# A conditional residual block on one core: beta of every fourth group by DMA, b2 by GpSimd, and a later load of x

## The chip, the cores and the metric

The kernel runs on one core of a Trainium2 chip. The metric is the device time of one execution in microseconds. The kernel before takes 313.89 us (median of 3 runs, 313.76 to 314.14). A core has five engines that work side by side, each on its own queue of instructions: PE (TensorE, matmuls and transposes), DVE (VectorE), ACT (ScalarE), Pool (GpSimd) and SP (SyncE), which here only issues DMAs. An instruction waits for semaphores that other engines or DMAs raise; what stands behind it in the same queue waits with it.

## The reference

x has 128 batches of 128 rows by 512 columns. Each batch b has an id v (0 to 9) that picks one of ten sets of weights W1, b1, W2, b2, gamma, beta. For each batch:

```
h   = relu(x @ W1[v] + b1[v])            # 128 x 128
y   = x + h @ W2[v] + b2[v]              # 128 x 512
out = x + (y - mean(y)) * rsqrt(var(y) + 1e-5) * gamma[v] + beta[v]
```

Mean and variance go over the 512 columns. All data are float32.

## The kernel before

**Tiling.** The 128 rows of a batch are the partitions. x is loaded in groups of four batches (G = 4, 32 groups, 1 MB each) into a pool of four buffers (`xp`); out is stored in pairs of batches (512 KB each). W1, W2 and the rows of gamma, beta and b2, spread over all partitions (`gamma_b`, `beta_b`, `b2_b`), stay in SBUF.

**One batch.** PE transposes x (L218), multiplies by W1 (L241) and by W2 (L258). ACT copies the transposed x (L222), stages the batch's W1 (L209), applies relu (L249), and sums the squares (L288). DVE adds up y and its row sum (`residual`, L273), subtracts the mean and multiplies by gamma (`scale`, L322), and multiplies by the reciprocal deviation and adds a tile o (`finish`, L331). Pool makes two sums: r = x + b2 (`add_b2`, L228), which `residual` reads, and o = x + beta (`add_beta`, L235), which `finish` reads and overwrites with the result. SP issues the load of x (`load_x`, L68) and the store of o (`store`, L335).

**Three ways to add b2.** `b2_by_matmul` (the first four batches, and every batch with b % 4 == 1 that is not done by DVE; 22 in all): one more matmul into y's accumulation (L257), and `residual` reads x itself. `b2_by_vector` (b % 8 == 5 from 13 to 109; 13 in all): an add on DVE before `residual` (L271). All others (93): Pool makes r.

**Order.** One Python loop runs over i; with b = i - 3 it issues, in this order: the load of x three groups ahead (at the first batch of a group), transposes of batch b + 3, `add_b2(b + 2)`, `add_beta(b)`, the W1 product of b + 2, the W2 product of b + 1, then DVE's work for b and the two batches before it: `finish` and `store` are three batches behind `residual`. `keep` fixes that order on each engine. The stores are outside of it: the tile scheduler puts them where it thinks fit among SP's other instructions. The language ids are read into registers of each engine once per group (`lid`).

**Buffers.** r has four (`rp`), a pair's o five (`op`), x four, y five PSUM banks (`p_y`). A tile of a pool takes the buffer of the tile that stands as many places before it as the pool has buffers, and waits until that one's readers (for o: its store) are done.

**End.** The last four batches are finished in `tail`, in an order written out by hand. Pool has the last five big instructions of its own there: for batches 123 and 124 a multiplication by gamma (L384) and an add (L386), for 125 an add. The queue of Pool before them ends with the adds of beta for batches 125 to 127. The stores of single batches follow in order on SP (`store_last`, L389).

Of the kernel before, what the change touches and what calls it, by code (L numbers as in the profile page):

```python
# [8 lines left out]
FP = mybir.dt.float32  # L9
# [3 lines left out]
ALU = mybir.AluOpType  # L13
ET = mybir.EngineType
PSUM = bass.MemoryType.PSUM

P = 128
G = 4
# [6 lines left out]
def cond_resid_kernel(ctx: ExitStack, tc: tile.TileContext, x, itok, W1, b1, W2, b2, gamma, beta, out):  # L25
# [8 lines left out]
    nc = tc.nc  # L34
    B, S, H = x.shape
    L, _, A = W1.shape
    KC = H // P
    NG = B // G
# [5 lines left out]
    def keep(ins):  # L44

        engine = ins.ins.engine
        if engine in last:
            tc.add_manual_dep(ins.ins, last[engine], behind, reason="kept order")
        last[engine] = ins.ins.name
        return ins  # L50
# [1 line left out]
    const = ctx.enter_context(tc.tile_pool(name="const", bufs=1))  # L52
    xp = ctx.enter_context(tc.tile_pool(name="xp", bufs=4))
    rp = ctx.enter_context(tc.tile_pool(name="rp", bufs=4))
    op = ctx.enter_context(tc.tile_pool(name="op", bufs=5))
    tp = ctx.enter_context(tc.tile_pool(name="tp", bufs=2))
    wp = ctx.enter_context(tc.tile_pool(name="wp", bufs=3))
    st = ctx.enter_context(tc.tile_pool(name="st", bufs=6))
# [5 lines left out]
    xs = {}  # L64

    def load_x(g):
        t = xp.tile([P, G, H], FP, tag="x", name=f"x_{g}")
        keep(nc.sync.dma_start(out=t, in_=x[g * G : (g + 1) * G].rearrange("b s h -> s b h")))  # L68
        xs[g] = t

    def xb(b):
        return xs[b // G][:, b % G, :]
# [27 lines left out]
    for l in range(0, L, 5):  # L100
        keep(
            nc.sync.dma_start(
                out=w1e[:, l : l + 5].rearrange("p l k a -> p l (k a)"),
                in_=W1[l : l + 5].rearrange("l (p k) a -> p l (k a)", k=KC),
# [4 lines left out]
    def load_w1(k):  # L109
        keep(  # L110
            nc.sync.dma_start(out=w1[:, :, k, :], in_=W1[:, k * P : (k + 1) * P, :].rearrange("l p a -> p l a"))
        )

    for l in range(0, L, 5):
        keep(
            nc.sync.dma_start(
                out=w2[:, l * H : (l + 5) * H].rearrange("p (l h) -> p l h", l=5),
                in_=W2[l : l + 5].rearrange("l a h -> a l h"),
# [48 lines left out]
    beta_b = const.tile([P, L * H], FP, name="beta_b")  # L167
# [14 lines left out]
    lids, xT, w1s, hT, rs, os, ys, ssqs, nmeans, rstds = {}, {}, {}, {}, {}, {}, {}, {}, {}, {}  # L182
    phs, pxs, sums = {}, {}, {}

    def lid(b, engine):
        g = b // G
        if (g, engine) not in lids:
            loads, vals = nc.values_load_multi_w_load_instructions(
                lang[0:1, g * G : (g + 1) * G],
                engines=[engine],  # L190
                min_val=0,
                max_val=L - 1,
                skip_runtime_bounds_check_because="clamped on the chip to 0..L-1 above",
            )
            for ins in loads:
                keep(ins)
            lids[g, engine] = vals
        return lids[g, engine][b % G]

    def b2_by_matmul(b):  # L200
        return b < 4 or (b % 4 == 1 and not b2_by_vector(b))

    def b2_by_vector(b):
        return b % 8 == 5 and 8 <= b < B - 16

    def stage_w1(b):
        w1s[b] = wp.tile([P, KC, A], FP, tag="w1s", name=f"w1s_{b}")
        src = (w1e if b < EARLY else w1).rearrange("p l k a -> p (l k a)")[:, bass.ds(lid(b, ET.Activation) * (KC * A), KC * A)]
        keep(nc.scalar.copy(w1s[b].rearrange("p k a -> p (k a)"), src))  # L209

    def transpose_x(b):
        pxs[b] = p_x.tile([P, KC, P], FP, tag="xT", name=f"pxT_{b}")
        for k in range(KC):
            if b < EARLY:
                cols = xb(b).rearrange("s (p k) -> s k p", k=KC)[:, k, :]
            else:
                cols = xb(b)[:, k * P : (k + 1) * P]
            keep(nc.tensor.transpose(pxs[b][:, k, :], cols, ident))  # L218

    def copy_xT(b):  # L220
        xT[b] = tp.tile([P, KC, P], FP, tag="xT", name=f"xT_{b}")
        keep(nc.scalar.copy(xT[b], pxs.pop(b)))  # L222

    def add_b2(b):
        if not b2_by_matmul(b) and not b2_by_vector(b):
            rs[b] = rp.tile([P, H], FP, tag="r", name=f"r_{b}")
            v = lid(b, ET.Pool)
            keep(nc.gpsimd.tensor_tensor(rs[b], xb(b), b2_b[:, bass.ds(v * H, H)], ALU.add))  # L228

    def add_beta(b):  # L230
        g, j = divmod(b, 2)
        if j == 0:
            os[g] = op.tile([P, 2, H], FP, tag="o", name=f"o_{g}")
        v = lid(b, ET.Pool)
        keep(nc.gpsimd.tensor_tensor(os[g][:, j, :], xb(b), beta_b[:, bass.ds(v * H, H)], ALU.add))  # L235

    def down(b):
        phs[b] = p_h.tile([P, P], FP, tag="h", name=f"ph_{b}")
        for k in range(KC):
            keep(  # L240
                nc.tensor.matmul(  # L241
                    phs[b], lhsT=w1s[b][:, k, :], rhs=xT[b][:, k, :], start=(k == 0), stop=(k == KC - 1)
                )
            )
        del xT[b], w1s[b]

    def relu(b):
        hT[b] = tp.tile([P, P], FP, tag="hT", name=f"hT_{b}", bufs=6)
        keep(nc.scalar.activation(hT[b], phs.pop(b), AF.Relu, bias=b1T[:, bass.ds(lid(b, ET.Activation), 1)]))  # L249

    def up(b):
        v = lid(b, ET.PE)
        ys[b] = p_y.tile([P, H], FP, tag="y", name=f"py_{b}")
        m = b2_by_matmul(b)
        if m:
            pick_b = pick[:, bass.ds(v + 2 * L, 1)].to_broadcast([96, P])
            keep(nc.tensor.matmul(ys[b], lhsT=pick_b, rhs=parts[:96, :], start=True, stop=False))  # L257
        keep(nc.tensor.matmul(ys[b], lhsT=hT[b], rhs=w2[:, bass.ds(v * H, H)], start=not m, stop=True))  # L258
        del hT[b]
# [5 lines left out]
    def residual(b):  # L265
        r = rs.pop(b) if b in rs else xb(b)
        if b % 2 == 0:
            sums[b // 2] = st.tile([P, 2], FP, tag="sum", name=f"sum_{b // 2}")
        if b2_by_vector(b):
            v = lid(b, ET.DVE)  # L270
            keep(nc.vector.tensor_tensor(ys[b], ys[b], b2_b[:, bass.ds(v * H, H)], ALU.add))  # L271
        keep(
            nc.vector.scalar_tensor_tensor(ys[b], ys[b], 1.0, r, ALU.mult, ALU.add, accum_out=col(sums, b))  # L273
        )
# [28 lines left out]
    def rstd_1(g):  # L303
        y0s[g] = p_s.tile([P, 6], FP, tag="s", name=f"stat_{g}")
        keep(nc.vector.reciprocal(y0s[g][:, 0:2], sds[g]))  # L305
# [32 lines left out]
    def on(b):  # L338
        return 0 <= b < B
# [151 lines left out]

    for i in range(3, B + U):
        b = i - U - 1
        if b > 0 and b % G == 0 and b // G + 3 < NG:
            load_x(b // G + 3)
        if i == 5:
            load_x(3)
        if i in (4, 6, 8, 10):
            load_w1((i - 4) // 2)
        if i == 4:  # L500
            up(2)
        if i == 5:
            up(3)
        if i > 3 and on(i):
            transpose_x(i)
        if b <= E:
            add_b2(b + 2)
            add_beta(b)
        if i > 4 and on(i - 1):
            down(i - 1)  # L510
        if i > 3 and on(i):
            copy_xT(i)
        if i > 4 and on(i + 1):
            stage_w1(i + 1)
        if i > 4 and on(i - 1):
            relu(i - 1)
        if i > 5 and on(i - U):
            up(i - U)


        g, half = divmod(b, 2)
        p = g - 1
        mine, old = 0 <= p < B // 2, 0 <= p - 1 < B // 2
        if b == E:
            add_b2(b + 3)
            add_beta(b + 1)
            add_b2(b + 4)
            for n in range(b + 2, B):
                add_beta(n)
        if b > E:  # L530
            tail(b)
        elif half == 0:
            if on(b):
                residual(b)
            if mine:
                rstd_1(p)
                scale(2 * p)
            if on(b):
                negative_mean(b)
            if mine:  # L540
                rstd_2(p)
            if old:
                finish(2 * p - 1)
                store(p - 1)
            if mine:
                rstd_3(p)
        else:
            if on(b):
                residual(b)
            if mine:  # L550
                rstd_4(p)
                scale(2 * p + 1)
            if on(b):
                negative_mean(b)
            if mine:
                finish(2 * p)
        if 0 <= b <= E:
            square(b)
            if half == 1:
                deviation(g)  # L560

        for n, engine in ((i + 3, ET.Activation), (i - U + 3, ET.PE), (b + 1, ET.DVE), (b + 5, ET.Pool)):
            if on(n):
                lid(n, engine)
# [37 lines left out]
```

## Time and profile before

| | |
|---|---|
| median of 3 runs | 313.89 us (313.76 to 314.14) |
| the profiled execution | 313.83 us, of which the span of its instructions 312.1 us |
| granted TensorE clock, mean | 0.99 |
| PE busy | 300.5 us (96%), 1869 instructions |
| DVE busy | 297.3 us (95%), 945 |
| ACT busy | 285.4 us (91%), 724 |
| Pool busy | 280.1 us (90%), 234 |
| DMA | 75.49 MB, 242 GB/s over the span |

Busy is the time in which at least one instruction of an engine ran, and the share is an average over the whole span, the first 20 us of loading and the last 15 us included. Instructions of one engine overlap in their pipelines: a Pool add lasts 1274 ns in the mean, but the next starts 1233 ns after it. So the distance from start to start tells what an instruction costs, and the duration when its result is there. A DMA's time counts from its issue to its landing. L12 is line 12 of the kernel before; from L55 on the lines of the changed kernel have other numbers (L228 becomes L229, L235 becomes L254, L335 becomes L354).

### The profile page before, as it was taken

To read this page: it belongs to the slowest core of one execution; us is meant where nothing else is said; L and a number is where in the kernel's file an instruction comes from. 1 tells how busy PE (TensorE), PEld (TensorE's weight loads), DVE (VectorE), ACT (ScalarE), POOL (GpSimd) and SP (SyncE) were. 2 spreads that over 40 slices of the span, in tenths; PEclk is the share of its full clock that TensorE was granted. 3 is DMA by queue.
4 is the path that set the end of the run, shared out by engine and by line. 5 is a ranking of instruction groups with operands and counts; after the bars stand their busy time and mean duration, and the time that the engine had idled before them with its cause. 6 is when DMAs were issued, how large, how long until landed. Compare 5 with 4: busy or idle time off the path is not lost.

```text
span 312.1 us, 7096 instructions
## 1 busy us (share of the span) xinstructions
PE 300.5 (96%) x1869; PEld 223.8 (72%) x1869; DVE 297.3 (95%) x945; ACT 285.4 (91%) x724; POOL 280.1 (90%) x234
## 2 busy tenths in 40 slices
PE   8999999999999999999999999999999999999970
PEld 3567787777777767777777777777777777777740
DVE  6677999999999999999999999999999999999995
ACT  3878999999999999999999999999999999999982
POOL 1319978999999999999999999999999999999963
PEclk9999999999999999999999999999999999999995
DMA  6999998767776777667666567576666667633234
GB/s 209 387 387 352 326 339 275 238 229 226 236 250 225 255 265 269 242 231 270 257 227 226 210 238 253 213 272 269 232 232 198 232 247 239 244 134 138 88 149 168
DMA packets 42313, 75.49 MB, mean 242 GB/s; under 512 B 1785, under 2 KB 6916, under 8 KB 42274
## 3 DMA queue, kind: packets, MB, share of 16 engines
q1 hardware_dynamic: 42214, 75.00, 68.6%
q8 instruction: 15, 0.25, 0.3%
q14 instruction: 24, 0.20, 0.2%
q10 hardware_dynamic: 60, 0.05, 0.1%
HBM read 41.49 MB, written 33.55 MB: 240 GB/s over the span
## 4 chain that ended last, share of the span: by engine, by line
PE 91%; DVE 5%; ACT 1%; issue 1%; DVEq 1%; DMA 1%; ACTq 0%
PE ph L241 36%; PE py L258 34%; PE pxT L218 18%; PE py L257 1%; PE row L175 1%; DVE py L273 1%; DVE gamma_b L180 1%; DVE py L322 1%; DVE o L331 1%; DMA rows<-in_L_cond_b_dram 1%; ACT sq L366 0%; DVEq L597 0%; ACT n L382 0%; DVE left L156 0%; DVE left L154 0%
## 5 line engine op out<-in xcount | busy, mean ns | idle before, releaser
L235 POOL TENSOR_TENSOR o<-x,beta_b 128x512 f32<-128x512 f32 x128 | 161.6, 1274 | 12.8 <-ACT beta_b L178 9.2
L241 PE MATMUL ph<-xT,w1s 128*128 128x128 f32 x1024 | 135.6, 275 | 0.5 <-ACT w1s L209 0.5
L258 PE MATMUL py<-w,hT 128*128 x256 | 131.1, 594 | 0.0
L228 POOL TENSOR_TENSOR r<-x,b_b 128x512 f32<-128x512 f32 x93 | 118.5, 1274 | 11.5 <-DMA x<-in_x_dram 9.2
L241 PEld LDWEIGHTS ph<-xT,w1s 128*128 128x128 f32 x1024 | 124.7, 192 | 2.4 <-ACT w1s L209 1.0
L218 PEld LDWEIGHTS pxT<-ident,x 128*128 128x128 f32 x512 | 65.5, 148 | 64.9 <-issue 44.8
L322 DVE SCALAR_TENSOR_TENSOR py<-py,nmean,gamma_b 128x512 f32<-128x512 f32 x126 | 93.8, 745 | 0.2 <-issue 0.2
L331 DVE SCALAR_TENSOR_TENSOR o<-py,rstd,o 128x512 f32<-128x512 f32 x122 | 91.0, 746 | 0.0
L288 ACT ACTIVATE sq<-py,sum 128x512 f32<-128x512 f32 x124 | 85.3, 688 | 1.4 <-DVE py L273 1.3
L222 ACT COPY xT<-pxT 128x512 f32<-128x512 f32 x128 | 73.8, 577 | 9.8 <-PE pxT L218 6.3
L218 PE MATMUL pxT<-ident,x 128*128 128x128 f32 x512 | 77.4, 274 | 0.0
L209 ACT COPY w1s<-w 128x512 f32 x112 | 69.5, 621 | 0.0
L273 DVE SCALAR_TENSOR_TENSOR py<-py,r 128x512 f32<-128x512 f32 x93 | 64.6, 694 | 1.3 <-PE pxT L218 0.6
L249 ACT ACTIVATE hT<-ph,b1T 128x128 f32<-128x128 f32 x128 | 47.4, 370 | 1.0 <-PE ph L241 1.0
L258 PEld LDWEIGHTS py<-w,hT 128*128 128x128 f32 x256 | 40.6, 192 | 2.4 <-ACT hT L249 0.7
L273 DVE SCALAR_TENSOR_TENSOR py<-py,x 128x512 f32<-128x512 f32 x35 | 24.4, 697 | 1.6 <-ACT sq L288 0.6
L288 ACT ACTIVATION_READ_ACCUMULATOR sq<-py,sum 128x1 f32 x124 | 25.7, 208 | 0.0
L299 ACT ACTIVATE sd<-ssq,eps 128x2 f32<-128x2 f32 x62 | 18.3, 296 | 2.1
L279 DVE TENSOR_SCALAR nmean<-sum 128x1 f32<-128x1 f32 x128 | 19.5, 152 | 0.1
L305 DVE RECIPROCAL stat<-sd 128x2 f32<-128x2 f32 x62 | 13.0, 210 | 1.0 <-ACT sd L299 1.0
L273 DVE DVE_READ_ACCUMULATOR py<-py,r 128x1 f32 x93 | 13.4, 144 | 0.0
L317 DVE RECIPROCAL rstd<-stat 128x2 f32<-128x2 f32 x62 | 10.4, 168 | 0.0
(56 smaller groups left out, 120.6 us busy)
## 6 DMA issues: line engine op xcount, KB each, us to landing
out_dram<-o SPq DMA_DIRECT2D x61, 512.0 KB, 3.9
x<-in_x_dram SPq DMA_DIRECT2D x30, 1024.0 KB, 5.8
w1e<-in_L_cond_W_dram SPq DMA_DIRECT2D x2, 1280.0 KB, 8.7
w<-in_L_cond_W_dram SPq DMA_DIRECT2D x2, 1280.0 KB
w<-in_L_cond_W_dram SPq DMA_DIRECT2D x4, 640.0 KB, 15.2
x<-in_x_dram SPq DMA_DIRECT2D x4, 512.0 KB, 8.4
out_dram<-o SPq DMA_DIRECT2D x6, 256.0 KB, 2.0
rows<-in_L_cond_beta_dram ACTq DMA_DIRECT2D x1, 20.0 KB
```

The costliest lines, as they stand in the source:

```text
L209: keep(nc.scalar.copy(w1s[b].rearrange("p k a -> p (k a)"), src))
L218: keep(nc.tensor.transpose(pxs[b][:, k, :], cols, ident))
L222: keep(nc.scalar.copy(xT[b], pxs.pop(b)))
L228: keep(nc.gpsimd.tensor_tensor(rs[b], xb(b), b2_b[:, bass.ds(v * H, H)], ALU.add))
L235: keep(nc.gpsimd.tensor_tensor(os[g][:, j, :], xb(b), beta_b[:, bass.ds(v * H, H)], ALU.add))
L241: nc.tensor.matmul(phs[b], lhsT=w1s[b][:, k, :], rhs=xT[b][:, k, :], start=(k == 0), stop=(k == KC - 1))
L249: keep(nc.scalar.activation(hT[b], phs.pop(b), AF.Relu, bias=b1T[:, bass.ds(lid(b, ET.Activation), 1)]))
L258: keep(nc.tensor.matmul(ys[b], lhsT=hT[b], rhs=w2[:, bass.ds(v * H, H)], start=not m, stop=True))
L273: nc.vector.scalar_tensor_tensor(ys[b], ys[b], 1.0, r, ALU.mult, ALU.add, accum_out=col(sums, b))
L288: nc.scalar.activation(sq, ys[b], AF.Square, bias=col(sums, b), scale=-float(H), accum_out=col(ssqs, b))
L322: nc.vector.scalar_tensor_tensor(ys[b], ys[b], col(nmeans, b), gamma_b[:, bass.ds(v * H, H)], ALU.add, ALU.mult)
L331: nc.vector.scalar_tensor_tensor(o, ys.pop(b), rstds[g][:, j : j + 1], o, ALU.mult, ALU.add)
```

## The change

- In every fourth group (q % 4 == 3, up to group 27; seven groups) Pool makes no o = x + beta. Instead SP issues four DMAs of 256 KB that copy the four batches' beta rows from `beta_b` into a tile `od` of the whole group (`fill_beta`), five batches ahead; two batches ahead, Pool issues one DMA that adds the 1 MB of x onto it (`add_x`). `finish` and `store` use the halves of `od` like two tiles o.
- `od` has one buffer, and `op` has four instead of five.
- b2 is added by matmul in the first four batches alone (4 instead of 22), by DVE where b % 16 == 5, from 21 to 101 (6 instead of 13), and by Pool in all others (118 instead of 93).
- The load of x three groups ahead is issued at the third batch of a group instead of the first.

```diff
-    op = ctx.enter_context(tc.tile_pool(name="op", bufs=5))
+    op = ctx.enter_context(tc.tile_pool(name="op", bufs=4))
+    od = ctx.enter_context(tc.tile_pool(name="od", bufs=1))
...
     def b2_by_matmul(b):
-        return b < 4 or (b % 4 == 1 and not b2_by_vector(b))
+        return b < 4
 
     def b2_by_vector(b):
-        return b % 8 == 5 and 8 <= b < B - 16
+        return b % 16 == 5 and 8 <= b < B - 16
...
+    def beta_by_dma(q):
+
+        return q % 4 == 3 and q < NG - 2
+
+    def fill_beta(q):
+
+        o = od.tile([P, G, H], FP, tag="od", name=f"od_{q}")
+        os[2 * q], os[2 * q + 1] = o[:, 0:2, :], o[:, 2:4, :]
+        for j in range(G):
+            v = lid(q * G + j, ET.SP)
+            keep(nc.sync.dma_start(out=o[:, j, :], in_=beta_b[:, bass.ds(v * H, H)]))
+        return o
+
+    def add_x(q, o):
+        keep(nc.gpsimd.dma_start(out=o, in_=xs[q], accum_op=ALU.add))
+
     def add_beta(b):
         g, j = divmod(b, 2)
+        if beta_by_dma(b // G):
+            return
         if j == 0:
             os[g] = op.tile([P, 2, H], FP, tag="o", name=f"o_{g}")
...
     for i in range(3, B + U):
         b = i - U - 1
-        if b > 0 and b % G == 0 and b // G + 3 < NG:
+        if b > G and b % G == 2 and b // G + 3 < NG:
             load_x(b // G + 3)
...
         if i > 3 and on(i):
             transpose_x(i)
+        q, at = divmod(b + 5, G)
+        if at == 0 and beta_by_dma(q):
+            filled = fill_beta(q)
+        q, at = divmod(b + 2, G)
+        if at == 0 and beta_by_dma(q):
+            add_x(q, filled)
         if b <= E:
             add_b2(b + 2)
             add_beta(b)
```

In the changed kernel's built program, SP's instructions of one such group stand in this order (group 7; tile o_g is the pair of batches 2g and 2g + 1, od_q the four of group q):

```
load   x_8      waits for PE and Pool (the last readers of x_4: beta of batch 19 on Pool)
store  od_3     first half, waits for DVE
store  od_3     second half, waits for DVE
registers: the language ids of group 7
fill   od_7     waits for both stores of od_3
fill   od_7
fill   od_7
store  o_8      waits for DVE
fill   od_7
```

## The prediction

> **What bounds the kernel now.** I read the page first (busy shares, the chain that ended last, the costliest groups), then the timelines of PE and Pool in the middle and at the end, then the DMA view of single stretches. Busy shares and chain:
>
> ```profile
> PE 300.5 (96%) x1869; PEld 223.8 (72%) x1869; DVE 297.3 (95%) x945; ACT 285.4 (91%) x724; POOL 280.1 (90%) x234
> ...
> PE 91%; DVE 5%; ACT 1%; issue 1%; DVEq 1%; DMA 1%; ACTq 0%
> ```
>
> Four engines look full, but the chain that ended last is 91% PE. Matmul starts of the down-to-output product (PE timeline; start, us, engine, line):
>
> ```profile
> 73.63 1.02 PE L258 MATMUL py<-w,hT 128*128 x2
> 75.82 0.38 PE L257 MATMUL py<-parts,pick 96*128 96x512 bf16 x1
> 76.04 1.02 PE L258 MATMUL py<-w,hT 128*128 x2
> 78.23 1.02 PE L258 MATMUL py<-w,hT 128*128 x2
> ```
>
> A batch takes 2.19 us, to the hundredth, from batch to batch; one with b2 by matmul takes 0.22 more. PE sets the pace. The groups (busy us, mean ns, idle before) and the Pool timeline:
>
> ```profile
> L235 POOL TENSOR_TENSOR o<-x,beta_b 128x512 f32<-128x512 f32 x128 | 161.6, 1274 | 12.8 <-ACT beta_b L178 9.2
> L228 POOL TENSOR_TENSOR r<-x,b_b 128x512 f32<-128x512 f32 x93 | 118.5, 1274 | 11.5 <-DMA x<-in_x_dram 9.2
> ```
> ```profile
> 64.28 1.28 POOL L228 TENSOR_TENSOR r<-x,b_b 128x512 f32<-128x512 f32 x1
> 65.52 1.27 POOL L235 TENSOR_TENSOR o<-x,beta_b 128x512 f32<-128x512 f32 x1
> ...
> 293.72 1.27 POOL L228 TENSOR_TENSOR r<-x,b_b 128x512 f32<-128x512 f32 x1 [0.31 <-DVE stat L305]
> 294.96 3.73 POOL L235 TENSOR_TENSOR o<-x,beta_b 128x512 f32<-128x512 f32 x3
> 300.98 1.27 POOL L384 TENSOR_TENSOR n<-n,gamma_b 128x512 f32<-128x512 f32 x1 [2.28 <-ACT n L382]
> ...
> 304.93 2.48 POOL L386 TENSOR_TENSOR o<-n,o 128x512 f32<-128x512 f32 x2
> ```
>
> Pool's adds follow each other every 1.233 us without a gap. Seven of them per group are 8.63 us, against 8.76 of PE (8.98 with a b2 matmul): Pool keeps up by 1 to 4%. At the end it is held only by the four buffers of r: the add at 293.72 makes r of batch 127 and waits for DVE to finish with r of batch 122:
>
> ```profile
> 292.89 0.70 DVE L273 SCALAR_TENSOR_TENSOR py<-py,r 128x512 f32<-128x512 f32 x1
> ```
>
> So r's buffer comes free 0.83 us after its residual starts. Pool then has 2.28 us to spare before its last five instructions, which end at 307.41. Loads and stores (DMA view of two stretches: a load with a store issued 0.47 us behind it; two stores by themselves; KB each, us from issue to landing):
>
> ```profile
> x<-in_x_dram SPq DMA_DIRECT2D x1, 1024.0 KB, 5.8
> out_dram<-o SPq DMA_DIRECT2D x1, 512.0 KB, 6.7
> ```
> ```profile
> out_dram<-o SPq DMA_DIRECT2D x2, 512.0 KB, 3.2
> ```
> ```profile
> DMA packets 252, 0.52 MB, mean 397 GB/s; under 512 B 0, under 2 KB 0, under 8 KB 252
> ```
>
> A store behind a load lands 3.5 us later than alone; the last line is the rate while a load and the store behind it run, 170.0 to 171.3 us.
>
> **The Trainium skill.** GPSIMD Engine Reference, 2.1 and 3.1: a two-input add costs about 2.6 cycles per element at 1.2 GHz, by a shared read port; 512 elements are an estimated 1.11 us plus dispatch. The trace's 1.233 agrees, and it is the same in mid-kernel and at the end, so I let it stand after the change. DMA: Bandwidth & Descriptors, "Issuing engines are not separate DMA queues": all DMAs share the same 16 engines and interleave; 6.7 beside 3.2 agrees. Same page, "SWDGE vs HWDGE vs iDMA" and the latency table: an accumulating DMA must be issued from GpSimd, whose cores write the descriptors, and the first byte comes after about 1 us. No DMA of before is issued from Pool. SBUF — State Buffer ("A bandwidth-pool intuition that's wrong"): such a DMA took about 620 ns alone and 3100 ns when a DVE instruction held the shared port.
>
> **The change, part by part.** The unit is 16 batches, 16k to 16k+15: 35.04 us of PE without b2 matmuls, 35.48 with two.
>
> *PE.* 18 b2 matmuls go (22 to 4): 18 x 0.22 = 3.94 us less on the path. ACT and DVE allow that: ACT is unchanged at 38.4 of each 40 us, and DVE, working without a gap after a b2 add, does two batches in 4.24 us (160.00 to 164.24) against PE's 4.38. DVE loses 7 of 13 adds of 0.72 us (their start to the next start); it is hidden behind PE, worth nothing.
>
> *Pool adds.* b2: 93 to 118. beta: 128 to 100. Per 16 batches 15 + 12 = 27 adds x 1.233 = 33.3 us. Left of 35.04: 1.76 us, for one accumulating DMA (cost t on Pool) and any wait (w).
>
> *t.* Not in the trace. Low end 0.6, high end 3.1, by the page above. I take 1.2: the page's 1 us of emission, near one Pool add.
>
> *w: SP's queue.* In the built order SP has, once per 16 batches (k = 1): the load of x_8; both stores of od_3 (batches 12 to 15); three of the four fills of od_7; the store of o_8 (batches 16, 17); the fourth fill. Stores are not in the kept order and slipped behind the load, whose buffer waits for beta of batch 19. The fill waits until both od_3 stores have landed, as there is one od buffer. And Pool's beta of batch 24 needs o_8's buffer: with four o tiles and none used by a DMA group, o_12 follows o_8. Let P be the end of beta(19) on Pool.
> - SP: load at P+0.03 (the load at 90.24 followed the Pool add that ended at 90.21), stores at +0.5 and +0.97. Load plus one store landed 7.15 after the load's issue (0.47+6.7); one more store is 0.52 MB at 397 GB/s, 1.3 us: landed at P+8.5.
> - Fills at +8.55, 9.0, 9.45; store of o_8 at +9.9; alone it takes 3.2, so it lands at about P+13.0 (12.7 with the fastest store, 2.8; 13.75 if the three fills, 0.79 MB, all go first).
> - Pool: nine adds stand between (r22, beta20, r23, ... r26): ready for beta(24) at P+11.06.
>
> So w = 13.0 - 11.06 = 1.9 us (1.65 to 2.7). Behind the waiting add stand r27 to r31 and the accumulating DMA; DVE's residuals wait for these r's, then PE for its five py buffers. At most, r is ready 4 x 2.19 - 0.83 - 1.27 = 6.66 us early; that is eaten first.
>
> *Per 16 batches* Pool then takes 33.3+1.2+1.9 = 36.4, 1.34 more than PE. It happens at groups 7, 11, 15, 19, 23, 27: 6 x 1.34 = 8.0 us.
>
> *The tail.* From batch 112 every batch has both adds on Pool (2.47 us against 2.19). r(114) cannot start before residual(110)+0.83. Residual(110) at PE's pace: 292.89 - 12 x 2.19 - 2 x 0.22 = 266.17, less the 14 matmuls removed up to there (3.08): 263.09. From 263.92 on there are 30 adds to beta(127): 29 x 1.233 + 1.27, done at 300.95. The last five Pool instructions thus start no earlier than before (300.98), though PE and DVE come 3.94 us earlier; the 2.28 us to spare are gone. Pool ends at 307.41; then three stores follow, 0.43 apart, the last issued at 308.3 instead of 308.77. So even with t and w covered, 3.94 shrink to 0.47.
>
> *The rest.* The added 7 MB of fills and 7 MB of accumulation (reads its destination too) come to some 20 MB beside 75.5: 27% more, priced through w. The accumulation is issued about 14 us before finish needs it; 1 MB loads take 5.8, so I price it at 0, up to 1 us per group and us beyond 14. The x load two batches later has about 18 us until its transposes: 0.
>
> *Sum*, against the profiled 313.83 us (span 312.1 and 1.7 around it): -0.47 + 8.0 = 321.4. The median of the runs, 313.89, is 0.06 higher: 321.5.
>
> **Rivals.**
> 1. *All hidden but the tail* (t + w under 1.76): 313.83 - 0.47 = 313.4, which is within 0.2% (0.63 us, about what this kernel's measurements can tell from no change). For it: PE is the bound, and w is a difference of 1.9 between sums of 11 and 13. Against: it needs both at or below their low ends.
> 2. *Faster: PE's gain arrives whole*, 313.83 - 3.94 = 309.9. Mechanism: Pool's adds get quicker and it enters group 28 without a debt. Place: L235/L228 spacing; it decides below about 1.10 us (30 x 0.13 = 3.9). Against: 1.233 everywhere.
> 3. *The DMA on Pool is dear or transfers crowd*: t of 2.5 gives 313.4 + 6 x (2.5+1.9-1.76) = 329.2; with w at 3.5 too, 339. For it: the high end of 3.1, 27% more traffic in windows that already run at 397 GB/s.
> The change does do what it says: 18 matmuls and 28 beta adds go; 25 b2 adds, 28 fills and 7 accumulations come.
>
> **How the numbers follow.** Likeliest, Pool bound by t and w near 1.2 and 1.9: 0.54, 321.4, own range 316 (t 0.6, w 1.65) to 327. Rival 3: 0.25. Rival 1: 0.15, a small part of it just past 0.2%. Rival 2: 0.06. Range 313.3 to 331 leaves out rival 2 and half of rival 3. Faster 0.07, same 0.14, slower 0.79.
>
> **What would show it.** L257 falls to x4 and PE shows gaps before matmuls. Pool's L254 waits for out_dram about 2 us, six times, 11 us in all. SP waits for od's stores at L241. A Pool DMA row at L245 gives t. Pool is idle nowhere after 265 us and its last instruction ends after DVE's. Wrong if Pool's waits for stores are near 0, t is over 2, or the adds' spacing leaves 1.233.

## The result, and the profile after

The changed kernel takes 343.19 us (median of 4 runs, 341.57 to 345.29) against 313.82: a ratio of 1.0936, 95% interval 1.0912 to 1.096. The forecast was 321.4, with 331 as the upper end. The direction was right; the size was not, by 21.8 us. Ratios here compare the executions within 1.5% of the fastest of the same kernel; only the order run below had others.

The profiled execution took 342.52 us, its span 340.7 (before: 312.1). Busy shares and the chain that ended last:

```profile
PE 304.9 (89%) x1851; PEld 224.0 (66%) x1851; DVE 293.7 (86%) x938; ACT 287.9 (84%) x724; POOL 282.0 (83%) x238
...
PE 35%; POOL 18%; DVE 14%; issue 14%; DMA 12%; POOLq 3%; SPq 1%; DVEq 1%; ACT 0%; ACTq 0%
```

PE carried 91% of the chain before; now 35%. No engine is busy more than 89% of the span. The engines wait for each other. The groups say for what (busy us, mean ns, idle before and its releaser), then the view of the waits of Pool and SP (us in total, times, longest):

```profile
L254 POOL TENSOR_TENSOR o<-x,beta_b 128x512 f32<-128x512 f32 x100 | 131.2, 1321 | 44.4 <-DMA out_dram<-o 35.1
L229 POOL TENSOR_TENSOR r<-x,b_b 128x512 f32<-128x512 f32 x118 | 155.2, 1342 | 9.1 <-DMA x<-in_x_dram 9.1
```
```profile
POOL o L254 <- DMA out_dram<-o: 35.1, 12, 4.8
```
```profile
SPq L69 <- POOL o L254: 125.4, 14, 12.0
SPq L241 <- DMA out_dram<-od: 40.4, 6, 7.9
```

Pool's beta add waits 12 times, 35.1 us in all, for a store to land. SP waits for Pool before a load (L69), and for od's stores before the fills (L241). It also waits for the accumulating DMA before the load that takes over its x buffer:

```profile
SPq L69 <- DMA od<-x: 8.8, 7, 2.1
```

The loop of group 11 follows, 16 batches after the one that the prediction priced: P, the end of the beta add that the load waits for, is 104.81, and what is called x_8, od_3, od_7, o_8 and o_9 there is x_12, od_7, od_11, o_16 and o_17 here. First SP's queue, then Pool's:

```profile
104.84 0.38 SPq L69 DMA_DIRECT2D x<-in_x_dram  x1
105.32 0.97 SPq L354 DMA_DIRECT2D out_dram<-od  x2
113.54 1.80 SPq L241 DMA_DIRECT2D od<-beta_b  x3
115.43 0.54 SPq L354 DMA_DIRECT2D out_dram<-o  x1
116.11 0.50 SPq L241 DMA_DIRECT2D od<-beta_b  x1
116.77 0.85 SPq L69 DMA_DIRECT2D x<-in_x_dram  x1
117.67 1.39 SPq L354 DMA_DIRECT2D out_dram<-o  x2
```
```profile
118.76 1.28 POOL L254 TENSOR_TENSOR o<-x,beta_b 128x512 f32<-128x512 f32 x1 [2.90 <-DMA out_dram<-o]
...
122.42 0.87 POOL L245 DMA_DIRECT2D od<-x  x1
123.03 1.57 POOL L229 TENSOR_TENSOR r<-x,b_b 128x512 f32<-128x512 f32 x1
126.29 1.27 POOL L254 TENSOR_TENSOR o<-x,beta_b 128x512 f32<-128x512 f32 x1 [1.70 <-DMA out_dram<-o]
```

The order on SP is the forecast one. The first wait (2.90) is the forecast one too, an add that needs o_16's buffer. The second, at 126.29, is not in the prediction: the next pair's add needs o_17's buffer, and o_17's store (117.67) stands 0.9 us behind the load of x_13 (116.77), which stood behind the fills. The accumulating DMA holds Pool for 0.61 us (122.42 to 123.03). In the priced loop itself, of group 7 (P at 66.02), the first wait is 4.80 us and there is no second.

The DMA view from 104.5 to 119 us, in 40 slices of 0.36 us:

```profile
GB/s 0 0 0 34 85 34 56 119 56 305 395 424 350 379 356 373 429 384 435 379 435 384 345 28 0 0 0 0 322 379 390 384 345 384 384 401 379 345 362 209
```

For some 3 us after the load's issue little moves, then 345 to 435 GB/s, then for 1.5 us nothing: all of SP's transfers are done, and SP has only just been told that the fills may go (113.54). That second pause is a queue that waits, not transfers that crowd; what fills the first 3 us is not shown.

Where the 28.6 us between the two spans lie, by the starts of the W2 products of batches 16, 112 and 127 on PE:

| stretch | before | after | difference |
|---|---|---|---|
| start to batch 16 | 55.89 | 56.06 | +0.2 |
| batch 16 to 112 | 213.30 | 235.51 | +22.2 |
| batch 112 to 127 | 32.02 | 31.46 | -0.6 |
| batch 127 to the end | 10.9 | 17.7 | +6.8 |

### The profile page after: what moved, and what is told of

Its sections match the earlier page's. It is cut to its first block, busy times and chain, and to the rows that moved or that the text cites. A ratio compares the mean times of both kernels' runs of the same rounds, so it can differ in the third digit from the quotient of the medians.

```text
span 340.7 us, 7092 instructions
## 1 busy us (share of the span) xinstructions
PE 304.9 (89%) x1851; PEld 224.0 (66%) x1851; DVE 293.7 (86%) x938; ACT 287.9 (84%) x724; POOL 282.0 (83%) x238
## 2 busy tenths in 40 slices
DMA packets 47354, 90.17 MB, mean 265 GB/s; under 512 B 2346, under 2 KB 7477, under 8 KB 46419
## 3 DMA queue, kind: packets, MB, share of 16 engines
q0 software_dynamic: 1008, 7.34, 10.4%
## 4 chain that ended last, share of the span: by engine, by line
PE 35%; POOL 18%; DVE 14%; issue 14%; DMA 12%; POOLq 3%; SPq 1%; DVEq 1%; ACT 0%; ACTq 0%
PE py L277 14%; PE ph L260 13%; POOL r L229 8%; POOL o L254 7%; DMA od<-beta_b 7%; PE pxT L219 7%; DMA out_dram<-od 5%; DVE py L292 4%; DVE py L341 3%; DVE o L350 2%; POOLq L189 2%; POOL od L245 1%; PE row L176 1%; DVE od L350 1%; SPq L241 1%
## 5 line engine op out<-in xcount | busy, mean ns | idle before, releaser
L254 POOL TENSOR_TENSOR o<-x,beta_b 128x512 f32<-128x512 f32 x100 | 131.2, 1321 | 44.4 <-DMA out_dram<-o 35.1
L229 POOL TENSOR_TENSOR r<-x,b_b 128x512 f32<-128x512 f32 x118 | 155.2, 1342 | 9.1 <-DMA x<-in_x_dram 9.1
L277 PE MATMUL py<-w,hT 128*128 x256 | 134.9, 609 | 16.8 <-DVE o L350 16.2
L292 DVE SCALAR_TENSOR_TENSOR py<-py,r 128x512 f32<-128x512 f32 x118 | 81.6, 692 | 29.0 <-POOL r L229 25.3
L350 DVE SCALAR_TENSOR_TENSOR o<-py,rstd,o 128x512 f32<-128x512 f32 x94 | 69.8, 743 | 0.0
L277 PEld LDWEIGHTS py<-w,hT 128*128 128x128 f32 x256 | 39.0, 191 | 23.7 <-DVE o L350 21.6
L350 DVE SCALAR_TENSOR_TENSOR od<-py,rstd,od 128x512 f32<-128x512 f32 x28 | 20.8, 742 | 0.0
L292 DVE DVE_READ_ACCUMULATOR py<-py,r 128x1 f32 x118 | 16.6, 141 | 0.0
L336 DVE RECIPROCAL rstd<-stat 128x2 f32<-128x2 f32 x62 | 10.2, 165 | 0.0
```

The source lines that it names most:

```text
L350: nc.vector.scalar_tensor_tensor(o, ys.pop(b), rstds[g][:, j : j + 1], o, ALU.mult, ALU.add)
```

## The experiments

Theory A is the prediction's mechanism, made larger: a circle of Pool, SP's queue and the stores. A load waits for Pool; stores stand behind it; fills wait for stores, with one od buffer; the next stores stand behind the fills; and Pool, with four o buffers, waits for these. Theory B: the DMA on Pool (B1) or the added transfers (B2) cost the time by themselves. Theory C: the later load. Theory D: Pool is too full, and the waits are a symptom. (The tile names in the expectations are those of the prediction's loop, of group 7.)

**Five o buffers.**

```diff
-    op = ctx.enter_context(tc.tile_pool(name="op", bufs=4))
+    op = ctx.enter_context(tc.tile_pool(name="op", bufs=5))
...
-        hT[b] = tp.tile([P, P], FP, tag="hT", name=f"hT_{b}", bufs=6)
+        hT[b] = tp.tile([P, P], FP, tag="hT", name=f"hT_{b}", bufs=3)
...
-        sq = tp.tile([P, H], FP, tag="sq", name=f"sq_{b}")
+        sq = tp.tile([P, H], FP, tag="sq", name=f"sq_{b}", bufs=1)
```

> The changed kernel with five buffers for the pairs' o, as before the change (room made by three instead of six buffers of hT and one instead of two of the square's unused output). Theory A (a loop of Pool, SP's queue and the stores: the beta add of the first batches after a load waits for the store of the pair four o tiles earlier): with five buffers the add that waited 2.9 us needs o_7's elder, stored long before, and o_8's buffer is wanted 4 to 5 us later; Pool's 35.1 us of waits for stores fall below 8 us, one loop of 16 batches takes 33.3 + 0.6 = 33.9 us of Pool, under PE's 35.04, and the time is 313.4 to 317 us. Theory B (the accumulating DMA is dear on Pool, or the copies and accumulations crowd the transfers): the number of o buffers doesn't matter much, 335 us or more.

Measured: 322.64 us (320.82 to 324.36), ratio 1.0262 [1.0219, 1.0306]. One buffer gives back 20.6 of the 29.4 us. (hT and sq shrink with it; the last run has both small, and PE keeps its pace there.) Pool's waits for stores are gone altogether, but the time is above A's 317. Pool's waits in this run:

```profile
POOL od L245 <- DMA od<-beta_b: 13.6, 4, 4.1
...
POOL od L245 <- issue: 4.2, 3, 2.4
```

A wait took the place of the one removed: the fills still wait for od's stores (SP, 45.3 us), so they land late, and now Pool stands still before its accumulating DMA. That DMA lands late in turn, and SP's loads wait 29.0 us for it (8.8 in the changed kernel). A holds, but the circle has a second branch.

**Two od buffers, four of o.** Room comes from hT, sq, the staged W1 (two instead of three) and the ids' scratch rows.

```diff
-    od = ctx.enter_context(tc.tile_pool(name="od", bufs=1))
+    od = ctx.enter_context(tc.tile_pool(name="od", bufs=2))
```

> The changed kernel with two buffers for od, so that the fills needn't wait for the stores of the od before (room made by fewer buffers of hT, the square's output and the staged W1). o keeps four buffers. Theory A: SP no longer waits 6 times 7 us before the fills; the store of o_8 is issued when DVE is done with it, near the load and before the fills have all gone, and lands at about 11 us after the load's issue instead of 13.9; Pool's first wait per loop falls from 3 to about 0.5 us, the second from 2 to about 1, the time is 316 to 324 us. Theory B (traffic or the DMA on Pool itself): 338 us or more, since all transfers are still there.

Measured: 327.6 us (two runs), ratio 1.044 [1.0403, 1.0477]. Pool's waits for stores:

```profile
POOL o L254 <- DMA out_dram<-o: 22.0, 9, 5.0
```

SP's wait before the fills is gone, and with it 15.6 us, while all transfers are still there: this speaks for A against B. The size is a miss (first waits per loop 1.7 to 3.7 us, not 0.5): in the loop of group 11 the store of o_16 went out 5.5 us after the load instead of 10.6, but behind a load, two stores and four fills it took about 8 us to land.

**No accumulation.**

```diff
     def add_x(q, o):
-        keep(nc.gpsimd.dma_start(out=o, in_=xs[q], accum_op=ALU.add))
+        pass
```

> The changed kernel without the seven DMAs that add x onto od (so x is missing from the output of those 28 batches). Everything else stays, the fills and their waits too. Theory A: only the 0.61 us of Pool per loop and some store traffic goes: Pool still waits for stores, 25 us or more in all, and the time is 333 to 340 us. Theory B1 (the DMA issued from Pool, its descriptors or its reads and writes, costs the 29 us): 313 to 318 us.

Measured: 340.37 us (two runs), ratio 1.0847 [1.0825, 1.0869]. Without the seven DMAs only 2.8 us are gained, and Pool waits longer:

```profile
POOL o L254 <- DMA out_dram<-o: 38.5, 13, 4.6
```

35.1 became 38.5: most of what Pool saves it spends waiting for the same store. B1 is out.

**No fills** (all but the first four).

```diff
-        o = od.tile([P, G, H], FP, tag="od", name=f"od_{q}")
+        if q == 3:
+            filled_once.append(od.tile([P, G, H], FP, tag="od", name="od_3"))
+        o = filled_once[0]
...
-        for j in range(G):
+        for j in range(G if q == 3 else 0):
```

> The changed kernel with the four fills of the first od alone; the other six groups' fills are left out, so their output has what od held before instead of beta. The seven accumulating DMAs stay. Theory A: nothing on SP waits for od's stores any more, the store of o_8 goes out right behind them and lands before Pool wants its buffer; Pool's waits for stores fall below 10 us and the time is 313 to 319 us. Theory B1 (the DMA on Pool): 335 us or more. This and the run with two od buffers tell the fills' wait (A) from the fills' transfers (B2, the copies crowd the transfers: gain here, none with two od buffers).

Measured: 318.71 us (two runs), ratio 1.0157 [1.0133, 1.018]. The waits for stores (the beta add is L258 there) are a little above the expected 10 us; 4.32 of them lie at the start:

```profile
POOL o L258 <- DMA out_dram<-o: 11.0, 8, 4.3
```

Beside the run with two od buffers: 24.5 us go when the fills are left out, 15.6 when they need not wait. The remaining difference can be their transfers or their place ahead of the store in SP's queue; the order run below settles that.

**The later load alone**, in the kernel before.

```diff
-        if b > 0 and b % G == 0 and b // G + 3 < NG:
+        if b > G and b % G == 2 and b // G + 3 < NG:
```

> The kernel before with only the later load of x (third batch of a group instead of the first). Theory A and the prediction: about 18 us remain until the first transposes of that group, so nothing changes, 313.4 to 314.2 us. Rival C (the later load itself delays x): Pool or PE waits for x in mid-kernel, 316 us or more.

Measured: 313.88 us (12 runs), ratio 1.0 [0.9991, 1.0008]. The later load costs nothing by itself, so C is out.

**b2 moved to Pool alone**: the changed kernel without beta by DMA, with five o buffers.

```diff
     def beta_by_dma(q):
-        return q % 4 == 3 and q < NG - 2
+        return False
```

> The changed kernel without the DMAs for x + beta (no fills, no accumulation, all beta adds on Pool, five buffers of o): only the move of b2 to Pool and the later load are left. Pool then has 31 adds x 1.233 = 38.2 us per 16 batches against PE's 35.04, and 246 adds in all, 303 us: 333 to 343 us under any theory that holds the add at 1.233 us, with no waits for stores. If it is near 313, Pool has room that the prediction didn't see.

Measured: 347.96 us (two runs), ratio 1.1084 [1.1062, 1.1106]: 5 us above the expected span of 333 to 343. Here too Pool waits for stores, which was not expected (the beta add is L253 there):

```profile
POOL o L253 <- DMA out_dram<-o: 10.7, 7, 3.3
```

The median store of a pair lands 7.7 us after its issue in this run, without any fill or od; before the change it was 3.9. So a Pool that is the bound gets into a circle of loads and stores by itself, with five buffers of o.

**The order on SP alone.** All buffers as in the changed kernel, all transfers there.

```diff
-        nc.sync.dma_start(out=out[2 * g : 2 * g + 2].rearrange("b s h -> s b h"), in_=os.pop(g))
+        keep(nc.sync.dma_start(out=out[2 * g : 2 * g + 2].rearrange("b s h -> s b h"), in_=os.pop(g)))
...
-        if b > G and b % G == 2 and b // G + 3 < NG:
-            load_x(b // G + 3)
...
-        q, at = divmod(b + 5, G)
+        q, at = divmod(b + 7, G)
...
             add_x(q, filled)
+        if b > G and b % G == 3 and b // G + 3 < NG:
+            load_x(b // G + 3)
```

> The changed kernel, all buffers as they are, with another order on SP alone: stores take their place in the kept order, the fills are issued seven batches ahead instead of five, and the load comes one batch later, behind the fills. So no store of od or of o_8 stands behind a load that waits for Pool. Theory A: the stores of od land about 3 us after DVE is done with them, the fills don't wait 7 us, the store of o_8 is out before them; Pool's waits for stores fall from 35 to 10 us or less, 313.4 to 320 us. Theory B (transfers or the DMA on Pool cost the time by themselves): the same transfers are there, so 335 us or more.

Measured: 13 runs, median 316.0 us: six of 313.66 to 314.65, one of 316.0, six of 318.5 to 319.74. The ratio, 1.0014 [0.9997, 1.0031], is of the seven up to 316.0; the profiled execution took 318.82. Pool waits for no store at all in it. Busy time of each engine in stretches of the changed kernel, one for each loop (us, then PE, weight loads, DVE, ACT, Pool; granted clock, DMA share, GB/s):

```profile
95.00:134.00 39.00, 36.41 (x225) 27.07 (x226) 35.32 (x114) 34.93 (x90) 34.41 (x30) 1.00 0.89 273
175.00:214.00 39.00, 36.34 (x228) 27.14 (x228) 34.20 (x111) 34.37 (x89) 33.08 (x29) 1.00 0.83 264
214.00:253.00 39.00, 36.20 (x224) 26.85 (x224) 34.81 (x114) 34.34 (x89) 34.03 (x29) 1.00 0.85 268
```

The same view of the order run:

```profile
96.00:131.00 35.00, 35.00 (x226) 26.57 (x225) 34.97 (x116) 34.06 (x89) 34.08 (x29) 1.00 0.94 299
166.00:201.00 35.00, 35.00 (x226) 26.57 (x225) 34.93 (x114) 34.07 (x89) 34.12 (x29) 1.00 0.93 300
201.00:236.00 35.00, 35.00 (x226) 26.57 (x225) 34.90 (x114) 34.07 (x89) 34.05 (x29) 1.00 0.93 303
```

The stretches are cut to the loop's length in each run (the changed kernel's five are 38 to 41 us long). The same work (about 225 matmuls as counted there, 29 or 30 Pool instructions) takes 35 us instead of 39, and PE never stops. The transfers are the same and run at 300 GB/s instead of some 270. This is the run that decides: with the order alone changed, batches 16 to 112 take 210.3 us, against 235.5 in the changed kernel and 213.3 before, where 12 b2 matmuls more stand in that stretch (2.6 us). So B2 is out, and the whole loss of the middle lay in the order of one queue. In this execution one hole is left, near the start (PE timeline): x_4's load, one batch later, stands behind the last W1 load. Whether the quicker executions have that hole is not shown.

```profile
54.14 1.08 PE L219 MATMUL pxT<-ident,x 128*128 128x128 f32 x4 [4.21 <-DMA x<-in_x_dram]
```

**Beta by DMA alone**: b2 split as before the change.

```diff
     def b2_by_matmul(b):
-        return b < 4
+        return b < 4 or (b % 4 == 1 and not b2_by_vector(b))
...
-        return b % 16 == 5 and 8 <= b < B - 16
+        return b % 8 == 5 and 8 <= b < B - 16
```

> The changed kernel with b2 split as before the change (22 by matmul, 13 by DVE, 93 by Pool): only beta by DMA, the buffers and the later load are left. Pool has 24 adds per 16 batches, 29.6 us, and 5.9 us of room against PE's 35.48. Theory A: Pool is not full, but the loop holds all the same: from the load to the beta add of batch 24 13.9 us, then 16 adds (19.7), 0.6 and a second wait of 2: 36.3 us, 0.8 over PE; Pool waits 40 us or more for stores, 316 to 323 us. Rival D (the change is slow because Pool is too full, and the waits are only a symptom): 313 to 314.5 us.

Measured: 317.05 us (two runs), ratio 1.0099 [1.007, 1.0129], inside A's span. Pool waits less than the 40 us expected, with 5.9 us of room per loop:

```profile
POOL o L254 <- DMA out_dram<-o: 29.8, 11, 5.8
```

D is out as the sole cause: a Pool that isn't full waits for stores nearly as long (35.1 us in the changed kernel), and the kernel still loses 3 us. But with a full one the same circle costs 29.

**The end.** First the order run with x_4 loaded at the first batch of group 1 and the first fill five batches ahead:

```diff
-        if at == 0 and beta_by_dma(q):
+        if b == 7 or (at == 0 and q > 3 and beta_by_dma(q)):
+            q = max(q, 3)
...
-        if b > G and b % G == 3 and b // G + 3 < NG:
+        if (b == G or (b > 2 * G and b % G == 3)) and b // G + 3 < NG:
```

> The order run again, with the start as before: x_4 is loaded at the first batch of group 1 and the first fill is issued five batches ahead, since in the order run x_4 stood behind the last W1 load and PE waited 4.2 us for it at 50 us. All the rest as in the order run (4 o buffers, 1 od buffer, stores in the kept order, loads behind the fills). Theory A with the prediction's tail (from batch 112 Pool has both adds of every batch, so that the end can't come earlier than 0.47 us): no hole at 50 us, no waits of Pool for stores, 313.0 to 314.0 us. If the tail step was wrong, PE's whole gain of 3.94 us shows: 310 us. Theory B: unchanged, 335 us or more (already hard to hold).

and the same with four b2 matmuls at the end:

```diff
-        return b < 4
+        return b < 4 or (b >= 112 and b % 4 == 1)
```

> The same with b2 by matmul in batches 113, 117, 121 and 125, as before the change: Pool has 7 instead of 8 adds in each of the last four groups. 14 matmuls less than before, 14 x 0.22 = 3.08 us. If the tail step is right, that gain now reaches the end: 310.6 to 311.6 us, faster than both kernels, and PE is the bound to the end. If something else held the end in the run without it, 313 us or more.

Measured: 316.01 us (1.0056 [1.0037, 1.0074]) and 313.15 (0.9979 [0.9965, 0.9993]). Both miss by a new hole at the start, at 49 to 54 us: the first fills, among the W1 loads, take 7.5 us to land, and Pool stood 7.1 us (7.0 in the second) before the first accumulating DMA. Between each other they settle the tail. Pool's last instructions without the four matmuls, and with them:

```profile
300.65 3.73 POOL L254 TENSOR_TENSOR o<-x,beta_b 128x512 f32<-128x512 f32 x3
304.32 1.28 POOL L403 TENSOR_TENSOR n<-n,gamma_b 128x512 f32<-128x512 f32 x1
```
```profile
299.36 2.50 POOL L254 TENSOR_TENSOR o<-x,beta_b 128x512 f32<-128x512 f32 x2 [0.35 <-DVE py L292]
302.26 1.27 POOL L403 TENSOR_TENSOR n<-n,gamma_b 128x512 f32<-128x512 f32 x1 [0.40 <-ACT n L401]
```

Without them Pool works without a pause into its last five instructions: from the last W2 product to the end 14.1 us pass (301.12 to 315.2; before the change 10.9). With them Pool waits for ACT again, it is 10.7 us, and the kernel is 2.86 us faster though PE has 0.88 us more to do.

**The start.** Two more, to see whether a kernel faster than both is left. The first: beta by DMA from group 7 on, more b2 matmuls at the start, the first four stores out of the kept order.

```diff
-        return b < 4 or (b >= 112 and b % 4 == 1)
+        return b < 4 or (b % 4 == 1 and (b < 16 or b >= 112))
...
-        return q % 4 == 3 and q < NG - 2
+        return q % 4 == 3 and 3 < q < NG - 2
...
-        keep(nc.sync.dma_start(out=out[2 * g : 2 * g + 2].rearrange("b s h -> s b h"), in_=os.pop(g)))
+        ins = nc.sync.dma_start(out=out[2 * g : 2 * g + 2].rearrange("b s h -> s b h"), in_=os.pop(g))
+        if g >= 4:
+            keep(ins)
```

> The run with the tail's matmuls, with a start as before the change: beta by DMA from group 7 on (six groups), b2 by matmul in the batches with b % 4 == 1 below 16 too, x_4 loaded at the first batch of group 1, and the first four stores left out of the kept order, so that the W1 loads don't wait behind them. In the two runs before it Pool stood still for 7 us at 42 to 50 us, since the first fills landed 7.5 us after their issue among the W1 loads, and PE waited 2.9 us for that. 11 matmuls less than before, 11 x 0.22 = 2.42 us. If the hole at 50 us was all that was left, 311.2 to 311.8 us; if transfers disturb the middle as well, 312.5 or more.

Measured: 315.64 us, 1.006 [1.0043, 1.0076], a miss of about 4 us. The hole at 50 us is gone, but Pool stood 7.2 us at 36 to 43 us, before a beta add of the fifth pair, and PE fell 3.0 us behind its pace of 2.19 us per batch from 85.35 to 99.32. The reading was that four o buffers are too few at the start as well: the profile puts Pool's wait down to DVE, but the first store, issued at 34.19, landed 8.7 us later, and Pool went on at 43.02. The second run has five of them (room as in the first experiment), and gives Pool seven adds per group up to batch 27:

```diff
-    op = ctx.enter_context(tc.tile_pool(name="op", bufs=4))
+    op = ctx.enter_context(tc.tile_pool(name="op", bufs=5))
...
-        return b < 4 or (b % 4 == 1 and (b < 16 or b >= 112))
+        return b < 4 or (b % 4 == 1 and (b < 28 or b >= 112) and not b2_by_vector(b))
...
-        return b % 16 == 5 and 8 <= b < B - 16
+        return b == 13 or (b % 16 == 5 and 8 <= b < B - 16)
```

> The run with the start as before, with five o buffers (room made by three instead of six buffers of hT and one for the square's unused output) and b2 split as before up to batch 27, so that Pool has seven adds per group until beta by DMA begins. In the run with four o buffers Pool stood still for 7.2 us at 36 to 43 us, since the first store lands 8.7 us after its issue and the fifth pair needs its buffer; with two adds per batch in batches 16 to 27 it had lost its lead by 62 us, and PE lost 2.3 us at 85 to 97. 10 matmuls less than before, 2.2 us. If that was the cause, no gaps of PE over 2.45 us before the tail and 311.4 to 312.0 us, faster than before by 0.6 to 0.7%; if transfers still hold PE up in the middle, 313 or more.

Measured: 311.42 us (311.4 to 311.87), ratio 0.9924 [0.9911, 0.9938]: faster than before the change by 0.76%. Its chain:

```profile
PE 88%; DVE 7%; issue 1%; ACT 1%; DVEq 1%; DMA 1%; ACTq 0%
```

PE sets the pace again, to the end: ten b2 matmuls less were to give 2.2 us, and the median is 2.4 lower. Two things changed together in this run; which of them the start needed is not shown.

## Why the prediction was right or wrong

**What failed: the working of w, "SP's queue".** Its order, its two waits (the fills for od's stores, the add for a store) and Pool's side were right: in the loop shown the fills started at P+8.7 (forecast 8.55) and Pool was ready at P+11.05 (forecast 11.06). The failing step is the size, 1.9 us per loop, in three terms. (1) The fills are issued 0.65 us apart, not 0.45: over three fills that is 0.6 us. The spacing had been taken from stores, whose issue lasts 0.42 to 0.46 us for od's in this loop; a fill's lasts 0.50, with a register instruction of 0.05 before it. What makes up the rest is not shown. (2) The landing: in this loop the store landed 3.27 us after its issue (forecast 3.1), in the priced one 4.9; and in the loop whose load is issued at 183.79 od's stores took until P+10.4. Why they differ is not shown. So the first wait was 2.9 to 4.8 us, mean 3.9. (3) The working stopped at the first waiting add. It had written down that four o tiles rotate, and priced only o_8; the next pair's buffer, o_9, is stored behind the next load, which the fills had pushed back. That second wait was put at nothing without a reason; it is 0.75 to 2.4 us, in five loops 7.3. Six loops cost 30.6 us of waiting, not 11.4: of the 19.2 missing, 11.9 are the first waits and 7.3 the second. A twelfth wait (4.5 us) fell at the start.

**The sum again.** 313.36 with all hidden but the tail; plus 30.6; less Pool's slack, 6 x (35.04 - 33.3 - 0.61) = 6.8: 337.2. The twelfth wait can add up to 4.5, so 341.7 at most, against 342.5 profiled. In PE's times, the middle lost 22.2 us and the end 6.8. From 284.32, the last wait, to the last five instructions at 329.82 Pool worked without a pause, so that what it had lost by then came out at the end.

**t was too dear.** 1.2 was taken, 0.61 measured from start to start (0.87 until its end). The Trainium skill's latency table (DMA: Bandwidth & Descriptors, "Latency and other measured facts") has about 1 us until the first byte of a DMA issued from GpSimd; here Pool was held for less than that. The low end came from the skill's 620 ns for a whole DMA alone (SBUF — State Buffer, "A bandwidth-pool intuition that's wrong"), which is another quantity: this DMA lands 7.3 to 10.2 us after its issue. That 0.6 came near the 0.61 was luck; 3.1 us was seen in no run. Rival 3 came nearest in size with 329 to 339 us, also by luck, since it named the wrong culprits: neither the DMA on Pool (2.8 us when left out) nor crowded transfers (35 us per loop with all of them) was the reason.

**The tail was right.** Pool from batch 112 on has too much to do, so PE's gain can't reach the end. In the run with x_4 early, r(114) was held by DVE:

```profile
267.40 1.28 POOL L229 TENSOR_TENSOR r<-x,b_b 128x512 f32<-128x512 f32 x1 [0.78 <-DVE stat L324]
```

29 x 1.233 + 1.27 later is 304.43, and the first of the last five started at 304.32. One slip stands in the working: between batches 110 and 122 three b2 matmuls stand (113, 117, 121), not two, so the earliest start of r(114) is 263.70 instead of 263.92, and the tail lets some 0.7 us of PE's gain through instead of 0.47. The run's start had cost 3.7 us against that; 313.1 + 3.7 = 316.8, and its profiled execution took 316.98.

**Right:** PE's pace and the 0.22 us of a b2 matmul (the middle of the order run goes at 35.05 us per 16 batches; the last run, with ten matmuls less, is 2.4 us faster); the adds' spacing, still 1.233 us; the later load, worth 0; the accumulation, which landed 7.3 to 10.2 us after its issue, in time for `finish`. That it also holds x's buffer, so that SP's loads wait for it (8.8 us in all), the prediction did not see. DVE's seven adds were hidden, but barely: it is busy 34.9 of 35 us there. The traffic grew by 14.7 MB (75.49 to 90.17), not 20, as the profile counts it: 7.34 MB for the accumulations, and as much for the fills.

**The range** left out half of rival 3. With two unknowns in w (spacing, landing) and a second buffer in the same rotation, its upper end for w, 2.7 us, was not a bound.

## What to carry to other kernels

When an engine waits for a buffer, price all tiles of that rotation, not only the first, and follow the queue through which they are freed to the next thing that stands in it: here it was a circle of four (adds, load, fills, stores), where removing one wait gave another its place, and work taken out of it (the accumulation) came back as waiting. A queue that issues both loads which wait for an early engine and stores which a late engine feeds should have its order written out; that alone brought 343 us to between 314 and 320, with the same buffers and the same bytes. And before giving a nearly full engine more to do in the last batches, look at the end by itself: what is hidden in the middle may set the end.

## What the runs showed that was not expected

- Idle DMA engines in a kernel that looks crowded: after a load's issue at 104.84 little moved for some 3 us, then 345 to 435 GB/s, then nothing for 1.5 us. The order run moved the same bytes at 300 GB/s through the middle.
- Pool adds last 1.26 to 1.57 us in the changed kernel (1.44 to 1.50 from 99.64 to 114.42), but still start every 1.233 us; the group's mean (1321 ns against 1274) says nothing on the pace.
- A fill of 256 KB within SBUF lands 2.3 to 3.5 us after its issue in the middle of the changed kernel, and among the W1 loads 6.8 us after it there, 7.5 in the run with x_4 early.
